# A gated scan followed by a mixture of experts: two norms on GpSimd, the first norm in one piece, and idle matrix time filled with unused products

## The chip, the cores and the metric

The kernel runs on one core of one Trainium2 chip. The metric is device time in microseconds (us), the median of several runs. Profiles are of one execution; TensorE is called PE, VectorE DVE, ScalarE ACT, GpSimd POOL and SyncE SP, as the profile calls them.

## The reference, cut to what matters

Input `x` has 4096 tokens of 128 channels, in 16 sequences of 256.

```python
# first half: a gated linear recurrence along each sequence
n  = layernorm(x)
it = sigmoid(n @ Wi.T + bi);  rt = sigmoid(n @ Wr.T + br)
at = exp(-8.0 * softplus(cap_lambda) * rt)
gx = sqrt(1.0 - at**2) * (it * n)
h[t] = at[t] * h[t-1] + gx[t]          # 256 steps, every channel by itself
x  = x + layernorm(h)
# second half: 32 experts, of which each token uses its 4 best
n  = layernorm(x)
scores = sigmoid(n @ gate_w.T)
ids    = top_k(scores + e_bias, 4);  w = scores[ids] / sum(scores[ids])
a[e]   = silu(n @ w1[e]) * (n @ w3[e]) * w[e]      # w1, w3: 128 x 96
x  = x + layernorm(sum over e of a[e] @ w2[e])     # w2: 96 x 128
```

## The kernel before

**Tiling.** The tokens are eight chunks (`CH`) of 512. For every chunk the piece `mix(c)` does the first half and the routing: normalise (`xn`), transpose (`xnT`), two gate products (`pr`, `pi`), the gates on ACT (`gr`, `gi`, `root`), the scan on DVE (`hs`), a transpose back (`back`), the norm `b`, the sum into `x_all`, the norm `c` (tile `hn`), a transpose (`hT`), the router product (`pl`), its scores and the choice of four experts.

**Two ways through the experts.** Six chunks, in the groups (0, 2, 3) and (4, 5, 6), go by tokens. `send` scatters the 512 x 4 rows of a chunk to the rows of their experts in DRAM with 16 indirect DMAs on POOL (`rows_in`, L507). When all 48 of a group are sent, `loads` brings blocks of 128 rows back on SP's queue (`xb`, L908), `experts` works on four blocks at a time (PE tiles `xT_ps`, `gu`, `aT_ps`, `y_ps`; ACT and DVE between them) and stores them (`rows_out`, L976). When all blocks of a group are stored, `fetch` gathers each token's four results with indirect DMAs on POOL (`yk`, L1044; 48 for a group), DVE weighs and adds them, and `combine` does the last norm and the store. Chunks 1 and 7 are dense: `dense(d, k)` runs all experts over a whole chunk in 24 blocks of 128 hidden units, products `dg`, `du`, `dw` (L1111) and `acc` (L1135), and `finish(d)` does the norm and the store (L1167). POOL's whole program is the setup at the start, the 96 scatters and the 96 gathers.

**The order.** Each piece is a Python generator that yields the engine and an assumed cost of its next step. `Order.run` takes, again and again, the step that can begin first on its own clock; among steps for one engine that begin within `SOON`, the one with the lowest due time goes first. This fixes the order of PE, DVE, ACT and SP; POOL's follows from it. Due times come from constants: chunk `c` is due at `LEAD + STEP * c`, experts from `full` on by `PACE`, dense blocks by `DUE` and `DDUE` (the last dense chunk by `DUE2`), always last on PE. `LND` and `CPD` are the assumed DVE costs where a step may go to ACT or DVE (`EITHER`); `STAY` puts off a step that makes ACT load another table. `AHEAD` goes into `in_pace`: a scatter or gather waits for the latest PE block product that the plan has at least `AHEAD` us earlier. `KEEP` is the number of blocks of the last dense chunk that may run before the last expert blocks have begun:

```python
        if d == len(DENSE) - 1 and k >= KEEP:
            yield UNTIL, lambda: 0.0 if began[-1] * QB >= NW[-1] else None
```

**The norms.** `rsqrt` is nine small DVE instructions (a shift-and-subtract guess and two Newton steps), each a step of its own, so others can be put between them. The first norm `a` has two pieces: `norm(range(1))` for chunk 0 and `norm(range(1, 8))` for the rest, and both are ready at once. For a name listed in `POWS`, `rsqrt` does an add and a power on POOL instead; the list is empty.

**Things in DRAM and weights.** SP's queue first loads `x_all`, clears the first group's rows, and then loads weights (`w`, `w_all`, `w_sb`) one piece after each of certain steps of `mix` (`some_later`).

Of the kernel before, what the change touches and what calls it, by code (L numbers as in the profile page):

```python
# [11 lines left out]
I32 = mybir.dt.int32  # L12
U32 = mybir.dt.uint32
AF = mybir.ActivationFunctionType
ALU = mybir.AluOpType
# [3 lines left out]
P = 128  # L19
EPS = 1e-5  # L20
K = 4
GROUPS = ((0, 2, 3), (4, 5, 6))
DENSE = (1, 7)
# [5 lines left out]
PE, DVE, ACT, POOL, SP, TIME = "pe", "dve", "act", "pool", "sp", "time"  # L29
# [7 lines left out]
class Order:  # L37
# [14 lines left out]
    def give(self, *names):  # L52
        for name in names:
            self.slots[name].append(self.now)
# [20 lines left out]
    def due(self, rank, step):  # L75
        due, n = rank
        if isinstance(due, dict):
            due = due.get(step[0], due[None])
        return due + STAY * self.switches(step), n

    def run(self, pieces):
# [8 lines left out]
        while live:  # L90
# [14 lines left out]
            if kind in (PE, DVE, ACT, POOL, SP):  # L105
                soon = [r for r in ready if r[3][0] == kind and r[0] <= begin + SOON]
                begin, _, p, step = min(soon, key=lambda r: self.due(r[1], r[3]))
# [19 lines left out]
                live.remove(p)  # L127


POWS = ()  # L130
POOLW = 0.9
RATE = 1.29
AHEAD = 3.0
READ = 0.0
LAST = 2
TINY = 0.07
SOON = 0.1
STAY = 6.0
LEAD, STEP, PACE = 38.0, 13.0, 0.6
DUE = 70.0  # L140
DDUE = 1.0
DUE2 = 200.0
LND, CPD = 1.7, 0.9
FLY2 = 3
KEEP = 6
MORE = 20
REGS = 3
SBANKS = 6
# [2 lines left out]
SLOT, UNTIL = "slot", "until"  # L151
# [3 lines left out]
def tile_gated_scan_then_moe(  # L155
# [30 lines left out]
    nc = tc.nc  # L186
# [3 lines left out]
    N = B * T  # L190
    TPC = 4
    CH = TPC * P
# [6 lines left out]
    NW = [min(n, t * K // P + MORE) for n, t in zip(NB, TG)]  # L199
    QB = 4  # L200
# [21 lines left out]
    def bank(name, dtype=F32):  # L222
        return psum.tile([P, CH], dtype, tag="bank", name=name)
# [128 lines left out]
    spread = const.tile([3 * E, UB * P], BF16, name="spread")  # L352
# [4 lines left out]
    for dst, src, rows in ((wiT, wi_in, P), (wrT, wr_in, P), (gwT, gw_in, E)):  # L357
# [5 lines left out]
    order = Order({  # L363
        "w": TILES - HELD, "ps": 8, "m": 3, "s": SBANKS, "d": 6, "acc": 2, "a": 4,
        "xb": 5, "regs": REGS, "blk": BLK, "yb": 4, "hn": HELD, "last": 3, "res": 1, "find": 2, "yk": 10,
    })
    give = order.give
# [11 lines left out]
    def rsqrt(rstd, var, pool, name):  # L379

        shape = [P, rstd.shape[1]]
        if name in POWS:
            v = pool.tile(shape, F32, tag="newt_v", name=f"nv_{name}")
            yield POOL, POOLW
            nc.gpsimd.tensor_scalar(v, var, EPS, None, ALU.add)
            nc.gpsimd.tensor_tensor(rstd, v, mhalf.to_broadcast(shape), ALU.pow)
            return  # L390
        v = pool.tile(shape, F32, tag="newt_v", name=f"nv_{name}")
        t = pool.tile(shape, F32, tag="newt_t", name=f"nt_{name}")
        yield DVE, TINY
        nc.vector.tensor_scalar(v, var, EPS, None, ALU.add)
        yield DVE, TINY
        nc.vector.tensor_scalar(
            t.bitcast(I32), v.bitcast(I32), 1, None, ALU.arith_shift_right
        )
        yield DVE, TINY
        nc.vector.tensor_scalar(  # L400
            rstd.bitcast(I32), t.bitcast(I32), -1.0, float(0x5F1FFFF9), ALU.mult, ALU.add
        )
        k = 0.703952253
        for square, plus in ((-1.0, 2.38924456), (-0.5 * k**3, 1.5 * k)):
            yield DVE, TINY
            nc.vector.scalar_tensor_tensor(t, rstd, square, rstd, ALU.mult, ALU.mult)
            yield DVE, TINY
            nc.vector.tensor_tensor(t, t, v, ALU.mult)
            yield DVE, TINY
            nc.vector.scalar_tensor_tensor(rstd, t, plus, rstd, ALU.add, ALU.mult)  # L410

    def moments(src, name, pool):

# [26 lines left out]
    times = {}  # L440
# [48 lines left out]
    def in_pace(ins):  # L489

        old = [b for at, b in beats if at <= order.now - AHEAD]
        if old:
# [6 lines left out]
    def send(g, cg):  # L499

        c = GROUPS[g][cg]
        yield UNTIL, lambda: times["rows", c][0] if ("rows", c) in times else None
        _, rows, hn = times["rows", c]
        for j in range(TPC):
            for k in range(K):
                yield POOL, RATE
                ins = nc.gpsimd.indirect_dma_start(  # L507
                    out=rows_in[g],
                    out_offset=bass.IndirectOffsetOnAxis(ap=rows[:, j, k : k + 1], axis=0),
                    in_=hn[:, j, :], in_offset=None,  # L510
                )
                apart(ins, f"in_{g}")
                in_pace(ins)
                sent[g].append(ins)
        times["sent", g] = order.now
        yield TIME, 2.5
        give("hn")
# [5 lines left out]

    def norm(chunks):

        for c in chunks:
            yield DVE, 1.1
            stats = small.tile([P, TPC, 6], F32, tag="stats_a", name=f"st_a{c}")
            for j in range(TPC):
                nc.vector.bn_stats(stats[:, j, :], x_all[:, c * TPC + j, :])  # L530
            for j in range(TPC):
                nc.vector.bn_aggr(mv_a[:, c * TPC + j, :], stats[:, j, :])
        span = slice(chunks[0] * TPC, (chunks[-1] + 1) * TPC)
        yield from rsqrt(rstd_a[:, span], mv_a[:, span, 1], const, f"a{chunks[0]}")
        yield DVE, TINY
        nc.vector.scalar_tensor_tensor(
            shift_a[:, span], mv_a[:, span, 0], -1.0, rstd_a[:, span], ALU.mult, ALU.mult
        )
        for c in chunks:
            times["normed", c] = order.now  # L540
# [8 lines left out]
    def decays():  # L549


        yield DVE, 0.4
        nc.vector.tensor_scalar(nabs, cap, -1.0, None, ALU.mult)
        nc.vector.tensor_tensor(nabs, nabs, cap, ALU.min)
        yield ACT, 0.2, "first exp"
        nc.scalar.activation(y, nabs, AF.Exp)
        yield DVE, 0.5
        nc.vector.tensor_scalar(u, y, 1.0, None, ALU.add)
        nc.vector.tensor_scalar(um1, u, 1.0, None, ALU.subtract)
        nc.vector.tensor_scalar(isz, um1, 0.0, None, ALU.is_equal)  # L560
        yield ACT, 0.2, "ln"
        nc.scalar.activation(lnu, u, AF.Ln)
        yield DVE, 1.2
        nc.vector.tensor_tensor(lnu, lnu, isz, ALU.add)
        nc.vector.tensor_tensor(um1, um1, isz, ALU.add)
        nc.vector.reciprocal(um1, um1)
        nc.vector.tensor_tensor(y, y, um1, ALU.mult)
        nc.vector.tensor_tensor(y, y, lnu, ALU.mult)
        nc.vector.tensor_scalar(decay, cap, 0.0, None, ALU.max)
        nc.vector.tensor_tensor(decay, decay, y, ALU.add)  # L570
        nc.vector.tensor_scalar(decay, decay, -4.0, None, ALU.mult)
        for b in (bi_sb, br_sb):
            nc.vector.tensor_scalar(b, b, 0.5, None, ALU.mult)
        times["decay"] = order.now
# [514 lines left out]
    def dense(d, k):  # L1089
# [3 lines left out]
        _, hT = times["hT", c]  # L1093
        if d == len(DENSE) - 1 and k >= KEEP:
            yield UNTIL, lambda: 0.0 if began[-1] * QB >= NW[-1] else None
# [75 lines left out]
    def spans(g, cg):  # L1171

        n = LAST if (g, cg) == (NG - 1, len(GROUPS[g]) - 1) else TPC
        return [(j, n) for j in range(0, TPC, n)]

    begun = set()
    w1_f, w3_f = (w13[:, i].rearrange("h e i -> h (e i)") for i in range(2))


    pieces = [(LEAD + STEP * c, mix(c)) for c in range(N // CH)]  # L1180
    pieces.append((0, norm(range(1))))
    pieces.append((-1, decays()))
    pieces.append((LEAD + STEP, norm(range(1, N // CH))))
    for g, chunks in enumerate(GROUPS):
        pieces += [(LEAD + STEP * c, send(g, cg)) for cg, c in enumerate(chunks)]
        full = LEAD + STEP * (chunks[-1] + 1)
        read = full + PACE * NW[g] + READ
        pieces.append((0, table(g)))
        pieces.append((0, loads(g, 0, NW[g])))
        pieces += [  # L1190
            (full + PACE * q, experts(g, q, NW[g])) for q in range(0, NW[g], QB)
        ]
        pieces += [
            (read + STEP * (cg + (j + n) / TPC), combine(g, cg, j, n))
            for cg in range(len(chunks)) for j, n in spans(g, cg)
        ]
        pieces += [(full + STEP * (cg + 1), find(g, cg)) for cg in range(len(chunks))]
        pieces += [
            (read + STEP * (cg + j / TPC), fetch(g, cg, j))
            for cg in range(len(chunks)) for j in range(TPC)  # L1200
        ]
    for d, c in enumerate(DENSE):
        pieces += [
            ({PE: 400 + d * UB + k, None: (DUE2 if d == len(DENSE) - 1 else DUE + DDUE * d * UB) + DDUE * k}, dense(d, k)) for k in range(UB)
        ]
# [13 lines left out]
    def step(piece, steps=None):  # L1219
# [14 lines left out]
    _, more_r = nc.values_load_multi_w_load_instructions(  # L1234
        more[0:1, 0:1], min_val=0, max_val=1,
        skip_runtime_bounds_check_because="0 or 1",
    )
# [42 lines left out]
```

## Time and profile before

| what | value |
|---|---|
| median of 3 runs | 376.28 us (375.01 to 378.33) |
| the profiled execution | 377.76 us, span 376.1 us |
| busy PE | 305.8 us (81%) |
| busy DVE | 290.7 us (77%) |
| busy ACT | 201.6 us (54%) |
| busy POOL | 195.4 us (52%) |
| mean granted PE clock | 0.927 |
| scatters on POOL, 96 | 66.3 to 213.5 us |
| gathers on POOL, 96 | 229.8 to 364.0 us |
| block loads on SP, 136 | 136.0 to 277.7 us |
| last store begins | 371.5 us |

A row of the timeline has the start and the length in us, the engine (with a q for its queue), the line of the kernel, the operation, output and inputs, the shapes, how many instructions are merged, and in brackets how long the engine was idle before and what ended that. A row of the stages has the stretch, its length, each engine's busy time and number of instructions, the granted PE clock (1 is full), and the DMA share and rate. PE ends are modelled.

### The profile page before, as it was taken

How to read it: one execution, taken by the hardware profiler on the slowest of the kernel's cores; microseconds unless marked ns; L12 is line 12 of the kernel's file. 1: busy time of each engine (PE TensorE's matmuls, PEld its weight loads, DVE VectorE, ACT ScalarE, POOL GpSimd, SP SyncE). 2: the span in 40 equal slices, each digit the busy share in tenths (PEclk: the TensorE clock that was granted, in tenths of full speed). 3: DMA queues.
4: the chain of work that ended last, by engine and by line, in shares of the span. 5: the costliest groups of instructions: out<-in, count | busy, mean ns of one | idle time of the engine just before them, and what ended most of it. 6: DMA issues, size and time to landing. Idle time of an engine off the chain costs nothing.

```text
span 376.1 us, 6098 instructions
## 1 busy us (share of the span) xinstructions
PE 305.8 (81%) x1423; PEld 199.2 (53%) x1423; DVE 290.7 (77%) x1252; ACT 201.6 (54%) x376; POOL 195.4 (52%) x220
## 2 busy tenths in 40 slices
PE   1095479799999998888889989877999999999900
PEld 0051254354543446777889956766999644444300
DVE  6955996989899998877874799637367488796993
ACT  2289897688677415457565546545466523141210
POOL 5000000772777727656737504776377767777750
PEclk9998657699999999899999999999699999999975
DMA  6906678362111124455545255667374522122231
GB/s 150 315 0 183 195 207 200 99 195 84 45 56 49 56 72 141 140 161 173 160 133 155 75 166 158 181 182 196 89 200 121 161 69 78 52 56 77 56 101 31
DMA packets 78856, 47.16 MB, mean 125 GB/s; under 512 B 15296, under 2 KB 75744, under 8 KB 78816
## 3 DMA queue, kind: packets, MB, share of 16 engines
q1 hardware_dynamic: 53808, 25.05, 24.3%
q0 software_dynamic: 6144, 12.60, 11.8%
q10 hardware_dynamic: 18864, 9.08, 8.2%
q8 instruction: 13, 0.21, 0.2%
q14 instruction: 27, 0.22, 0.2%
HBM read 23.76 MB, written 22.94 MB: 124 GB/s over the span
## 4 chain that ended last, share of the span: by engine, by line
PE 62%; DVE 12%; issue 5%; ACT 3%; POOL 2%; DMA 1%; DVEq 0%; POOLq 0%
PE gu L938 12%; PE acc L1135 10%; PE dg L1111 8%; PE y_ps L964 8%; PE du L1111 8%; PE aT_ps L954 4%; PE xT_ps L924 4%; PE dw L1111 2%; PE pl L675 2%; POOL yk L1044 2%; DMA yk<-rows_out,slots 1%; DVE a L1131 1%; DVE a L1123 1%; PE pr L600 1%; PE sw_c L448 1%
## 5 line engine op out<-in xcount | busy, mean ns | idle before, releaser
L507 POOL DMA_INDIRECT rows_in<-hn,rows x96 | 94.9, 988 | 113.2 <-DVE tot L481 60.8
L1044 POOL DMA_INDIRECT yk<-rows_out,slots x96 | 95.7, 996 | 54.8 <-issue 17.4
L938 PE MATMUL gu<-w,xT 128*128 x272 | 53.8, 336 | 7.9 <-issue 6.4
L1120 ACT ACTIVATE a<-dg 128x512 f32<-128x512 f32 x48 | 28.4, 596 | 49.7 <-PE dg L1111 49.2
L1135 PE MATMUL acc<-a,w_all 128*128 128x512 f32 x96 | 50.5, 617 | 3.3 <-DVE a L1131 1.4
L938 PEld LDWEIGHTS gu<-w,xT 128*128 128x128 f32 x272 | 44.6, 194 | 12.4 <-issue 7.7
L1111 PE MATMUL dg<-hT,w 128*128 128x512 f32 x96 | 50.7, 614 | 0.0
L1111 PE MATMUL du<-hT,w 128*128 128x512 f32 x96 | 50.0, 606 | 0.0
L946 DVE TENSOR_TENSOR act<-act,gu 128x192 f32<-128x192 f32 x68 | 23.0, 349 | 23.0 <-ACT act L944 22.5
L964 PE MATMUL y_ps<-w_sb,aT 96*128 x272 | 36.2, 280 | 5.3 <-issue 3.2
L1131 DVE TENSOR_TENSOR a<-a,dw 128x512 f32<-128x512 f32 x48 | 32.5, 681 | 9.1 <-PE dw L1111 8.6
L964 PEld LDWEIGHTS y_ps<-w_sb,aT 96*128 96x128 f32 x272 | 34.5, 196 | 8.5 <-issue 7.5
L1123 DVE TENSOR_TENSOR a<-a,du 128x512 f32<-128x512 f32 x48 | 32.4, 678 | 4.9 <-ACT a L1120 3.3
L944 ACT ACTIVATE act<-gu 128x192 f32<-128x192 f32 x68 | 22.0, 330 | 25.8 <-PE gu L938 21.6
L973 ACT COPY yb<-y_ps 128x512 f32<-128x512 f32 x34 | 19.9, 586 | 23.3 <-PE y_ps L964 22.3
L1135 PEld LDWEIGHTS acc<-a,w_all 128*128 128x128 f32 x96 | 17.1, 195 | 23.9 <-DVE a L1131 9.2
L1111 PEld LDWEIGHTS dg<-hT,w 128*128 128x128 f32 x96 | 18.3, 196 | 19.0 <-issue 17.3
L1111 PEld LDWEIGHTS du<-hT,w 128*128 128x128 f32 x96 | 17.7, 195 | 15.5 <-issue 14.0
L954 PE MATMUL aT_ps<-ident,act 128*96 128x128 f32 x136 | 20.4, 279 | 2.3 <-issue 1.6
L370 ACT COPY aT<-aT_ps 96x512 f32<-96x512 f32 x29 | 16.6, 583 | 9.4 <-PE aT_ps L954 8.1
L1054 DVE TENSOR_TENSOR yk<-yk,wk 128x512 f32<-128x512 f32 x24 | 16.5, 688 | 6.2 <-DMA yk<-rows_out,slots 6.0
L370 ACT COPY xT<-xT_ps 128x512 f32<-128x512 f32 x29 | 16.7, 588 | 7.0 <-PE xT_ps L924 6.1
(215 smaller groups left out, 520.9 us busy)
## 6 DMA issues: line engine op xcount, KB each, us to landing
xb<-rows_in SPq DMA_DIRECT2D x136, 64.0 KB
rows_out<-yb ACTq DMA_DIRECT2D x34, 256.0 KB
rows_in<-zeros SPq DMA_DIRECT2D x8, 512.0 KB
w<-in_L_ffn_w_dram SPq DMA_DIRECT2D x8, 384.0 KB
x_all<-in_L_attn_x_dram SPq DMA_DIRECT2D x8, 256.0 KB
w_all<-in_L_ffn_w_dram SPq DMA_DIRECT2D x4, 384.0 KB
w_sb<-in_L_ffn_w_dram SPq DMA_DIRECT2D x4, 384.0 KB
rows_in<-hn,rows POOLq DMA_INDIRECT x96
```

The lines of the kernel that those rows point to most:

```text
L370: (nc.vector.tensor_copy if kind == DVE else nc.scalar.copy)(dst, src)
L507: ins = nc.gpsimd.indirect_dma_start(out=rows_in[g], out_offset=bass.IndirectOffsetOnAxis(ap=rows[:, j, k : k + 1], axis=0), in_=hn[:, j, ...
L938: nc.tensor.matmul(pg[:, b, :], lhsT=xT[:, (h + b) * P : (h + b + 1) * P], rhs=w13[:, :, bass.ds(e, 1), :].rearrange("h s o i -> h s (o i) ...
L946: nc.vector.tensor_tensor(act[:, h : h + m, :], act[:, h : h + m, :], pg[:, :m, I : 2 * I], ALU.mult)
L954: nc.tensor.transpose(pa[:I, b * P : (b + 1) * P], act[:, b, :], ident)
L964: ins = nc.tensor.matmul(py[:, b, :], lhsT=aT[:, b * P : (b + 1) * P], rhs=w2_sb[:, bass.ds(e, 1), :].rearrange("i o h -> i (o h)"), start ...
L1044: ins = nc.gpsimd.indirect_dma_start(out=yk[:, k, :], out_offset=None, in_=rows_out[g], in_offset=bass.IndirectOffsetOnAxis(ap=rows[:, j, ...
L1111: ins = nc.tensor.matmul(ps, lhsT=lhsT, rhs=rhs, start=True, stop=True)
L1120: nc.scalar.activation(a, pg, AF.Silu)
L1123: nc.vector.tensor_tensor(a, a, pu, ALU.mult)
L1131: nc.vector.tensor_tensor(a, a, pw, ALU.mult)
L1135: nc.tensor.matmul(accs[d], lhsT=w2_all[:, k, :], rhs=a, start=(k == 0), stop=(k == UB - 1))
```

## The change

Two norms of the dense chunk 1 (`b1`, `c1`) go to POOL as powers. For chunk 0's norm `a` the nine instructions are one step, and the norm of the other chunks begins only after it. A new piece `warm` issues matrix products (96 x 128 by 96 x 512 in bf16) into one PSUM bank, which nothing reads, wherever the plan has PE idle, until the plan's clock is at 45. The last dense chunk's `mix` is due at 200 instead of 129, none of its blocks may go ahead of the last expert blocks, and several constants of the order differ. `LATER` is zero and changes nothing.

```diff
-POWS = ()
-POOLW = 0.9
+POWS = ("b1","c1")
+ATONCE = ("a0",)
+POOLW = 1.4
-AHEAD = 3.0
+AHEAD = 5.0
+WARM = 45.0
+MIXD = 200.0
+LATER = 0.0
-SOON = 0.1
-STAY = 6.0
-LEAD, STEP, PACE = 38.0, 13.0, 0.6
-DUE = 70.0
-DDUE = 1.0
+SOON = 0.12
+STAY = 8.0
+LEAD, STEP, PACE = 38.0, 11.0, 0.6
+DUE = 62.0
+DDUE = 2.0
-LND, CPD = 1.7, 0.9
+LND, CPD = 1.1, 0.7
-KEEP = 6
+KEEP = 0
...
+        def steps():
+            nc.vector.tensor_scalar(v, var, EPS, None, ALU.add)
+            yield
...                          # the same nine instructions as before
+        if name in ATONCE:
+            yield DVE, 1.7
+            for _ in steps():
+                pass
+            return
         yield DVE, TINY
+        for _ in steps():
             yield DVE, TINY
...
     def norm(chunks):
+        if chunks[0]:
+            yield UNTIL, lambda: times.get(("normed", 0))
...
+    def warm():
+        yield SLOT, "ps"
+        ps = bank("warm")
+        while order.now < WARM:
+            yield PE, 0.22
+            nc.tensor.matmul(
+                ps, lhsT=spread[:, :P], rhs=spread[:, :CH], start=True, stop=True
+            )
+        give("ps")
...
-    pieces = [(LEAD + STEP * c, mix(c)) for c in range(N // CH)]
+    pieces = [
+        (MIXD if c == DENSE[-1] else LEAD + STEP * c, mix(c)) for c in range(N // CH)
+    ]
+    pieces.append((1e6, warm()))
...
-            (full + PACE * q, experts(g, q, NW[g])) for q in range(0, NW[g], QB)
+            (full + PACE * q + LATER * g, experts(g, q, NW[g])) for q in range(0, NW[g], QB)
```

More of the change, by code (lines that the diff above doesn't have):

```diff
@@ L392, in rsqrt @@
         t = pool.tile(shape, F32, tag="newt_t", name=f"nt_{name}")
-        yield DVE, TINY
[L394 to L404, printed above, removed]
-            yield DVE, TINY
[L406 to L410, printed above, removed]
+        def steps():
+            nc.vector.tensor_scalar(v, var, EPS, None, ALU.add)
+            yield
+            nc.vector.tensor_scalar(
+                t.bitcast(I32), v.bitcast(I32), 1, None, ALU.arith_shift_right
+            )
+            yield
+            nc.vector.tensor_scalar(
+                rstd.bitcast(I32), t.bitcast(I32), -1.0, float(0x5F1FFFF9), ALU.mult, ALU.add
+            )
+            k = 0.703952253
+            for square, plus in ((-1.0, 2.38924456), (-0.5 * k**3, 1.5 * k)):
+                yield
+                nc.vector.scalar_tensor_tensor(t, rstd, square, rstd, ALU.mult, ALU.mult)
+                yield
+                nc.vector.tensor_tensor(t, t, v, ALU.mult)
+                yield
+                nc.vector.scalar_tensor_tensor(rstd, t, plus, rstd, ALU.add, ALU.mult)
+        if name in ATONCE:
[3 more added lines that the diff above has]
+            return
+        yield DVE, TINY
+        for _ in steps():
+            yield DVE, TINY
     def moments(src, name, pool):
@@ L1174, in spans @@
         return [(j, n) for j in range(0, TPC, n)]
+    def warm():
[5 more added lines that the diff above has]
+                ps, lhsT=spread[:, :P], rhs=spread[:, :CH], start=True, stop=True
+            )
+        give("ps")
     begun = set()
     w1_f, w3_f = (w13[:, i].rearrange("h e i -> h (e i)") for i in range(2))
-    pieces = [(LEAD + STEP * c, mix(c)) for c in range(N // CH)]
+    pieces = [
+        (MIXD if c == DENSE[-1] else LEAD + STEP * c, mix(c)) for c in range(N // CH)
+    ]
     pieces.append((0, norm(range(1))))
     pieces.append((-1, decays()))
+    pieces.append((1e6, warm()))
     pieces.append((LEAD + STEP, norm(range(1, N // CH))))
```

## The prediction

> **What bounds the kernel now.** I read the page's slices first, then the timeline of the start and of the end, then tables by stage.
>
> ```profile
> PE   1095479799999998888889989877999999999900
> DVE  6955996989899998877874799637367488796993
> ACT  2289897688677415457565546545466523141210
> POOL 5000000772777727656737504776377767777750
> ```
>
> A slice is 9.4 us. PE is nearly full from about 70 us to 358; the chain of waits gives PE 62% of the span. Before 70 us PE is not the bound: ACT is, from 20 to 60 us (37.6 us busy of 40 by stages). POOL is idle until its first scatter at 66.3. So what the start loses, the full PE stretch begins later by.
>
> ```profile
> 9.70 0.16 DVE L394 TENSOR_SCALAR nv_a<-mv_a 128x4 f32<-128x4 f32 x1
> 9.77 0.87 DVE L530 BATCH_NORM_STATS2 st_a<-x_all 128x6 f32<-128x128 f32 x4
> ...
> 17.31 0.16 DVE L536 SCALAR_TENSOR_TENSOR shift_a<-mv_a,rstd_a 128x4 f32<-128x4 f32 x1
> 17.51 1.65 ACT L377 ACTIVATE xn<-x_all,shift_a,rstd_a 128x128 f32<-128x128 f32 x4 [6.77 <-DVE shift_a L536]
> ...
> 25.26 0.69 ACT L607 ACTIVATE gr<-pr,br_sb 128x512 f32<-128x512 f32 x1
> ```
>
> Chunk 0's nine small instructions are strung out from 9.70 to 17.3 because the statistics of the other chunks (0.87 + 0.37 us each) stand between them; ACT waits 6.77 us for the end of it, and the first gate comes at 25.26.
>
> ```profile
> 34.30:44.50 10.20, 5.59 (x11) 2.27 (x10) 8.95 (x48) 9.93 (x14) 0.00 (x0) 0.50 0.73 203
> 44.50:47.90 3.40, 2.14 (x6) 0.57 (x5) 3.40 (x22) 1.97 (x5) 0.00 (x0) 1.00 0.68 196
> 47.90:61.60 13.70, 11.10 (x31) 6.99 (x31) 11.41 (x59) 13.53 (x19) 0.00 (x0) 0.50 0.94 239
> 61.60:68.40 6.80, 4.78 (x23) 2.14 (x21) 5.39 (x39) 2.71 (x6) 1.79 (x2) 1.00 0.31 90
> 68.40:75.20 6.80, 6.06 (x12) 2.70 (x13) 6.48 (x32) 4.80 (x8) 5.11 (x6) 0.50 0.42 127
> ```
>
> The stages show a PE at half clock in three stretches, the second being where the dense blocks begin.
>
> ```profile
> 56.34 3.76 PE L1111 MATMUL dg<-hT,w 128*128 128x512 f32 x4
> 59.89 2.73 PE L1111 MATMUL du<-hT,w 128*128 128x512 f32 x4
> 62.97 0.29 DVE L761 TENSOR_TENSOR places<-rank,filled 128x128 f32<-128x128 f32 x1 [3.15 <-PE rank L757]
> ```
>
> Chunk 0's ranking, which its first scatter needs, stood behind eight dense products that took 6.1 us instead of 3.4 (a pair at full clock is 0.86 in the chain).
>
> ```profile
> 303.16 0.94 POOL L1044 DMA_INDIRECT yk<-rows_out,slots  x1 [2.06 <-PE dw L1111]
> 363.09 0.95 POOL L1044 DMA_INDIRECT yk<-rows_out,slots  x1 [0.30 <-issue]
> 365.24 0.37 SPq L1167 DMA_DIRECT2D out_dram<-res  x1
> 371.48 0.37 SPq L1082 DMA_DIRECT2D out_dram<-ff  x1
> ```
>
> The end: the last group's blocks are stored at about 300, then 48 gathers at 1.25 to 1.27 us fill POOL to 364, and 12 us of weighing, norm and store follow. The last dense chunk's store begins 6.24 us ahead of the last one: that is its slack.
>
> **The change part by part.** Minus is earlier.
>
> *First norm.* Statistics of chunk 0 end at 6.75. The same nine instructions in a row take 1.75 us for norm b (36.67 to 38.42), so 8.5; three steps for the decay wait for ACT until 9.26 and end at 9.8; the shift ends at 10.0. With the lower assumed cost the scaling goes to DVE: eight took 2.14, so four 1.07, to 11.1. Transposes trail by 0.5, the copy is 0.6, the gate product at half clock 2.1: first gate at about 14.5, so -10.8 for chunk 0. The other chunks' statistics start later for it. DVE's work to the end of that norm is the same, less some 0.7 idle, plus the scaling 1.07 and chunk 0's early steps 2.6, so it ends near 23.5 instead of 20.7; with 3.5 us for scaling, transpose, copy and product, the next gate comes near 27 instead of 32.7. ACT has chunk 0's 6.8 us (0.69 + 0.82 + 0.71 + 0.64 + 0.72 + 0.63 and two table loads of 1.28) behind it by then. Bounds for the start of the dense blocks: 0, if ACT catches nothing up, to -10.8; I take -6, nearest to the second chunk's 5.7.
>
> *Powers.* Each takes nine DVE instructions (1.75) away and puts two on POOL, which is idle there. No power is in the trace. POOL's smallest rows are a memset of 0.10, the nearest of more work the two copies of 128x32 in 1.80: a norm costs 0.2 to 1.8, the two gain 3.1 to lose 0.1. I take 0.9 each, so 1.7 on chunk 1's chain, and count -1, as ACT is the bound there. If POOL were no longer idle, they would stand behind scatters of 1.26 us.
>
> *Unused products.* A pair of the like (`dw`) is 0.60, so one more costs 0.22, or 0.43 at half clock. The plan lays one per 0.47 us where PE has no other work; they delay a real product by 0.43 at most each, in a stretch that ACT bounds: cost 0, up to +1 if a bunch stands before a late transpose. They take one of eight banks until the dense blocks. Gain: 3.0 us at 56 to 62 if the clock is then full (eight products, 6.1 against 3.4, and the rank behind them), and as much as 2.7 more at 68 to 75, which they don't reach directly. Bounds -5.7 to +1; I take -3.
>
> The stages show what PE's clock needs: 81% busy from 47.9 to 61.6, much of it transposes and narrow products, and still half. [...]
>
> *KEEP and MIXD.* By tile, three blocks' `dg` and `du` and one `acc` of the last dense chunk ran from 213.5 to 291:
>
> ```profile
> 213.50:291.00 77.50, 2.96 (x6) 1.06 (x6) 1.70 (x3) 0.96 0.58 158
> 291.00:360.00 69.00, 21.45 (x42) 7.97 (x42) 12.50 (x21) 1.00 0.29 79
> ```
>
> (`dg`; 48 more instructions before.) That is 3 x 1.72 + 0.86 and some `dw`, 6.5 us of PE, moved behind the last group's blocks. Ahead of them it is worth -6.5 at most and nothing where it filled a wait; PE was 92% busy from 213.5 to 228, so I take -3. At the end it costs +6.5 against 6.24 of slack, so +0.3; up to +6.5 if DVE, 83% busy there (48.28 of 58.2), stretches it. Chunk 7's mixing, done at 226 until now, may slide; DVE has 28 us idle from 228 to 300, so I cost it at nothing.
>
> *AHEAD and the due times.* Scatters and gathers wait 8.3 and 14.7 us for PE products; 2 us of slack each can take away some of it. But the first group's gathers start when its blocks are stored, and the second's likewise, so 0, bounds -4 to +4 together with the changed dues, whose order no row shows.
>
> **Sum.** -6 - 1 - 3 - 3 = -13 for PE's full stretch. Not all reaches the end: PE carries 62% of the chain; the rest are other engines' steps and waits, the gathers at their own pace among them, that I leave as long as they are. So -13 x 0.62 = -8.1, +0.3, or -7.8: span 368.3, the profiled execution 370.0. That execution was 1.48 above the median, so the median becomes 368.5; I say 368.
>
> **The rivals.**
>
> *All of it arrives.* PE full from 60 on, looser pacing: -13 and -4, 359 to 363. For it: PE 93% busy from 70 to 213.5 (133.68 of 143.5). Against: gathers of the first group, 229.8 to 301, are the floor of the second's start; 48 at 1.25 leave only 11 us there.
>
> *The gain is given back.* Earlier scatters only wait longer for the next chunk's rows (POOL already waits 6.6 us at 94 and 6.2 at 140), as DVE (68.77 of 75.1 us busy from 75 to 150) sets chunks 2 to 6: 374 to 378. For it: DVE work falls by 3.5 us only.
>
> *The dense end decides, slower.* All 24 blocks of the last chunk need its `hT` and routing, and its `mix` now yields to everything until 200. A block is 0.86 x 3 + 0.22 = 2.8 us, 24 of them 67, the norm and store 7.3 + 4.6. If chunk 7 is ready later than the last expert blocks begin (about 291), each us goes to the end: 10 us late is 376.1 + 10 + 0.3, or 386. It decides from 4 us late on. Against: it would have to slide 65 us from 226.
>
> *Powers behind scatters.* If chunk 1's second norm comes after chunk 0's scatters are queued, it waits up to 16 x 1.26 = 20 us and the dense blocks start 13 later than now: 385. Now 15 us lie between (51 and 66.3); chunk 0 gains some 5 on chunk 1, so 10 remain. [...]
>
> **How the numbers follow.** Forecast 0.49 (its own range 362 to 374), all of it 0.18, given back 0.18, dense end 0.11, powers 0.04. A change under 1% (3.8 us) can't be told from none. Faster by over 1%, below 372.5: 0.67, all of the second and the forecast's. Within 1%: 0.18. Slower: 0.15, the last two. The range reaches from 358, past the largest gain, to 381, where the dense end is some 5 us late.
>
> **What would show it.** The first gate at 14 to 16; no half clock from 48 to 62; first dense product near 48; first scatter below 58; last scatter near 204, last gather near 355. Wrong if the first scatter moves by 8 or more and the last one stays at 213, or if `res` is the last store.

## The result, and the profile after

The changed kernel takes 379.58 us (median of four runs, 378.89 to 383.44), the one before beside it 376.73. The ratio is 1.011, with a 95% interval of 1.0065 to 1.0156: slower by 1.1%, where the prediction had it 2.1% faster. The profiled execution took 378.89 us with a span of 376.9.

Some executions are slower than the rest at a lower granted clock (of a_high, one took 382.82 us at 0.915 and one 374.23 at 0.945); a median here takes in all executions of a kernel and a ratio leaves those out, so that one median divided by another need not give the ratio.

The slices of the page of after:

```profile
PE   1998678999999688959799869777989999999940
DVE  7998899899889998947488986556858787888993
ACT  2599975876941124527355335434666332112110
POOL 5000187337557775174377037745666477777700
```

POOL starts its scatters two slices earlier than before. DVE is fuller at both ends (303.5 us busy against 290.7), ACT emptier (180.2 against 201.6). PE has more dips between 50 and 300 us.

The start, in the timeline of after (start, length, engine, line, operation):

```profile
8.88 5.30 PE L1198 MATMUL warm<-spread 96*128 96x512 bf16 x12
9.76 0.15 DVE L552 SCALAR_TENSOR_TENSOR shift_a<-mv_a,rstd_a 128x4 f32<-128x4 f32 x1
9.94 1.12 DVE L379 TENSOR_SCALAR xn<-x_all,rstd_a,shift_a 128x128 f32<-128x128 f32 x4
...
13.97 1.06 PE L462 MATMUL sw_a<-ident,xn 128*128 128x128 f32 x4
...
16.97 0.69 ACT L623 ACTIVATE gr<-pr,br_sb 128x512 f32<-128x512 f32 x1
```

The shift comes at 9.76 (17.31 before), the scaling lies on DVE, and the first gate comes at 16.97 instead of 25.26. Between the end of the scaling (11.06) and the transposes (13.97) lie 2.9 us; twelve unused products occupy PE from 8.88 to 14.18.

POOL, and the two DVE rows that compute where the next chunk's rows go, in the timeline of after:

```profile
42.83 1.05 POOL L393 TENSOR_TENSOR rs_b<-nv_b,mhalf 128x4 f32<-128x4 f32 x1
...
47.21 1.47 POOL L393 TENSOR_TENSOR rs_c<-nv_c,mhalf 128x4 f32<-128x4 f32 x1
48.88 1.25 POOL L521 DMA_INDIRECT rows_in<-hn,rows  x1 [0.21 <-issue]
...
79.63 0.17 DVE L490 TENSOR_SCALAR rows<-most 128x16 int32<-128x16 f32 x1
80.57 0.96 POOL L521 DMA_INDIRECT rows_in<-hn,rows  x1 [10.75 <-PE dg L1127]
...
157.38 0.17 DVE L490 TENSOR_SCALAR rows<-most 128x16 int32<-128x16 f32 x1
158.31 0.95 POOL L521 DMA_INDIRECT rows_in<-hn,rows  x1 [10.84 <-PE xT_ps L940]
```

The two powers are done before the first scatter, which starts at 48.88, 17.4 us earlier than before. Then POOL waits 10.8 us, twice. Nearly all of it is for the next chunk's row numbers (`rows`, ready at 79.8 and 157.6); the last 0.8 us are for the PE product that the written order has ahead of the scatter. The last scatter of the second group ends at 207.8, only 5.7 us earlier.

Two tables by stage of after (stretch, length, busy time and instructions of PE, weight load, DVE, ACT and POOL, clock, DMA share, GB/s):

```profile
47.90:59.77 11.87, 10.38 (x27) 6.10 (x28) 11.54 (x63) 8.44 (x13) 9.28 (x9) 0.57 0.84 215
...
210.00:240.00 30.00, 22.64 (x128) 17.86 (x127) 22.88 (x82) 11.74 (x24) 13.83 (x14) 0.94 0.51 137
240.00:295.00 55.00, 49.33 (x353) 46.07 (x352) 36.54 (x136) 29.78 (x65) 32.59 (x35) 0.97 0.62 169
```

Where the dense blocks begin the clock is again near half (0.57). Their first product stands at 53.87, against 56.34. From 210 to 295 PE is idle for (30 - 22.64) + (55 - 49.33) = 13.0 us; before it was 8.7 in the same stretches.

The end, in the timeline of after:

```profile
357.88 1.04 POOL L1060 DMA_INDIRECT yk<-rows_out,slots  x1 [0.31 <-issue]
...
362.49 1.12 PE L1151 MATMUL acc<-a,w_all 128*128 128x512 f32 x2 [1.19 <-DVE a L1147]
...
368.17 0.37 SPq L1098 DMA_DIRECT2D out_dram<-ff  x1
...
369.04 1.37 DVE L379 TENSOR_SCALAR res<-ff,rs_d,sh_d 128x128 f32<-128x128 f32 x4
372.77 0.69 DVE L1181 TENSOR_TENSOR res<-res,x_all 128x512 f32<-128x512 f32 x1 [2.37 <-DVEq L1268]
373.49 0.37 SPq L1183 DMA_DIRECT2D out_dram<-res  x1
```

This is the main reading. The kernel has two ends: the tokens' (last gather, then an `ff` store) and the dense one (last `acc`, then the `res` store of chunk 7). Before, the tokens' end was last: gathers to 364.0, `ff` at 371.5, `res` at 365.2. After, gathers end at 358.9 and `ff` is stored at 368.2, earlier by 5.1 and 3.3 us; but the last `acc` ends at 363.6 instead of 357.1, and `res` is stored at 373.5, later by 8.3. **The gain reached the tokens' end, and the dense end took its place.**

### The profile page after: what moved, and what is told of

The parts are those of the page before. It is cut to its first block, busy times and chain, and to the rows that moved or that the text cites. A ratio compares the mean times of both kernels' runs of the same rounds, so it can differ in the third digit from the quotient of the medians.

```text
span 376.9 us, 6241 instructions
## 1 busy us (share of the span) xinstructions
PE 317.0 (84%) x1488; PEld 205.9 (55%) x1488; DVE 303.5 (81%) x1278; ACT 180.2 (48%) x329; POOL 195.7 (52%) x224
## 5 line engine op out<-in xcount | busy, mean ns | idle before, releaser
L1060 POOL DMA_INDIRECT yk<-rows_out,slots x96 | 93.0, 969 | 58.1 <-issue 16.8
L954 PE MATMUL gu<-w,xT 128*128 x272 | 56.0, 347 | 11.6 <-issue 11.4
L954 PEld LDWEIGHTS gu<-w,xT 128*128 128x128 f32 x272 | 47.0, 203 | 14.3 <-issue 13.2
L1151 PEld LDWEIGHTS acc<-a,w_all 128*128 128x128 f32 x96 | 16.2, 189 | 29.1 <-DVE a L1147 20.4
L940 PE MATMUL xT_ps<-ident,xb 128*128 128x128 f32 x136 | 20.6, 281 | 1.3 <-issue 1.3
L970 PEld LDWEIGHTS aT_ps<-ident,act 128*96 128x96 f32 x136 | 16.0, 133 | 8.7 <-issue 5.6
L374 ACT COPY aT<-aT_ps 96x512 f32<-96x512 f32 x24 | 13.6, 584 | 14.4 <-PE aT_ps L970 14.1
```

The costliest lines, as they stand in the source:

```text
L954: nc.tensor.matmul(pg[:, b, :], lhsT=xT[:, (h + b) * P : (h + b + 1) * P], rhs=w13[:, :, bass.ds(e, 1), :].rearrange("h s o i -> h s (o i) ...
L970: nc.tensor.transpose(pa[:I, b * P : (b + 1) * P], act[:, b, :], ident)
L1060: ins = nc.gpsimd.indirect_dma_start(out=yk[:, k, :], out_offset=None, in_=rows_out[g], in_offset=bass.IndirectOffsetOnAxis(ap=rows[:, j, ...
L1151: nc.tensor.matmul(accs[d], lhsT=w2_all[:, k, :], rhs=a, start=(k == 0), stop=(k == UB - 1))
```

## The experiments

For each run: the ratio of its time to that of the kernel before, run beside it on the same chip, and times of its profiled execution, in us. A 95% interval is the range in which the ratio lies by the scatter of the executions. The profiled executions of a_oldlnd_keep6, b_newlnd and a_high were some 2.5 us above their medians, those of a_near1 and a_near2 2.3 and 3.2 us below, so their ends are late or early by some of that.

| kernel | ratio (95%) | first `dg` | last gather ends | last `acc` ends | `ff` store | `res` store | busy DVE / ACT |
|---|---|---|---|---|---|---|---|
| before | 1 | 56.3 | 364.0 | 357.1 | 371.5 | 365.2 | 291 / 202 |
| after | 1.011 (1.0065 to 1.0156) | 53.9 | 358.9 | 363.6 | 368.2 | 373.5 | 304 / 180 |
| a_keep6 | 1.0113 (1.007 to 1.0156) | 53.9 | 361.3 | 357.2 | 370.9 | 365.6 | 305 / 181 |
| a_oldlnd | 0.9887 (0.9853 to 0.992) | 52.5 | 353.4 | 356.3 | 362.8 | 363.4 | 292 / 195 |
| a_oldlnd_keep6 | 0.9824 (0.9773 to 0.9875) | 52.5 | 358.5 | 355.5 | 367.2 | 363.1 | 292 / 197 |
| a_lnd_only | 1.0006 (0.997 to 1.0042) | 52.9 | 358.1 | 361.5 | 368.0 | 368.6 | 299 / 190 |
| b_newlnd | 1.0253 (1.0202 to 1.0305) | 56.0 | 373.8 | 372.2 | 384.6 | 381.4 | 306 / 185 |
| a_frozen | 1.0221 (1.0176 to 1.0266) | 55.5 | 363.6 | 369.0 | 373.5 | 378.7 | 292 / 190 |
| o_frozen | 0.9879 (0.9821 to 0.9938) | 52.5 | 355.4 | 358.3 | 364.8 | 365.4 | 302 / 185 |
| a_near1 | 1.0197 (1.0146 to 1.0249) | 73.4 | 348.5 | 367.1 | 359.8 | 376.2 | 300 / 182 |
| a_near2 | 0.9923 (0.9887 to 0.9958) | 57.7 | 352.0 | 357.3 | 362.1 | 364.6 | 286 / 199 |
| a_high | 1.004 (1.0004 to 1.0076) | 57.9 | 364.1 | 364.2 | 373.7 | 373.0 | 284 / 208 |

**Parts undone or done alone.** The first theory was that `KEEP = 0` had made the dense end last, and that this was the loss.

```diff
 a_keep6, from after
-KEEP = 0
+KEEP = 6
```

> The changed kernel with KEEP back at 6 and nothing else undone. Theory 1 (the dense chunk's end decides: its 24 blocks stand behind the last expert blocks, and its last add behind the branch): three or more of its blocks go ahead again, its last store comes 6 us or more earlier, a store of ff is the last one, and the median is 374 to 376, 4 to 6 below the changed kernel's 379.6. Theory 2 (the gain of the start is given back before the end, between scatters and gathers): within 1.5 us of 379.6.

The time stayed: 378.97 us, 1.0113. Its end in the timeline:

```profile
360.34 0.94 POOL L1060 DMA_INDIRECT yk<-rows_out,slots  x1 [0.30 <-DMA yk<-rows_out,slots]
...
365.61 0.37 SPq L1183 DMA_DIRECT2D out_dram<-res  x1
370.88 0.37 SPq L1098 DMA_DIRECT2D out_dram<-ff  x1
```

The dense end did come back, its last `acc` by 6.4 us, but the last gather went 2.4 later and `ff` 2.7. What `KEEP` gives one end it takes in part from the other. Alone it decides nothing, and without it all the rest of the change moves the last store only from 371.5 to 370.9. So more than the dense end was wrong.

```diff
 a_silent, from after: the products are in the plan, and not issued
-            nc.tensor.matmul(
-                ps, lhsT=spread[:, :P], rhs=spread[:, :CH], start=True, stop=True
-            )
+            if order.now < 0.0:
+                nc.tensor.matmul(
+                    ps, lhsT=spread[:, :P], rhs=spread[:, :CH], start=True, stop=True
+                )
```

> The changed kernel with the same written order, in which the 65 unused products are planned but not issued; all real instructions keep their places. If the products earn their place by the clock: half clock again from about 30 to 48, first scatter 1 to 4 us later than 48.9, median 380 to 383. If they only stand in the way of real products: first scatter earlier by 1 or more, median 377 to 379. If PE does not bound the start: within 1 us of 379.6, first scatter within 1 us.

380.33 us, 1.0125 (1.0081 to 1.0169): not to be told from after. The first gate came earlier without the products (14.9, against 17.0), the first scatter later (50.6, against 48.9). From 34 to 50 us the mean clock was 0.67 without them and 0.98 with them; from 50 to 62, where the dense blocks begin, 0.59 and 0.60. They buy a full clock where they run and none behind it.

```diff
 a_nobranch, from after
-    with tc.If(more_r[0] > 0):
...                               # the fallback code at the end is left out
```

> The changed kernel without the branch at the end (the code for blocks beyond the planned number, which these inputs don't need, is left out). Theory 1: the last add of the dense chunk follows its scaling directly instead of 2.4 us later, and the median is 376 to 377.5, 2 to 3.5 below 379.6; gathers and everything before 360 unchanged. If the end of the program costs as much without the branch: within 1 us of 379.6.

378.74 us, 1.0117 (1.0062 to 1.0172). The gap of 2.4 us in front of the last addition (`DVEq L1268`) belongs to this code: without it `res` is stored 7.5 us behind the last `acc`, against 9.9. But taking it away gained nothing that can be told: the last `acc` came 2.0 us later in this run, and `res` was stored at 373.1 instead of 373.5.

```diff
 b_norm, from before: only the first norm in one step, and the order of the two pieces
+ATONCE = ("a0",)
...
+        if chunks[0]:
+            yield UNTIL, lambda: times.get(("normed", 0))
```

> The kernel before with only the first norm's change (nine instructions in one step, the other chunks' norm after it); all constants as before. If the early start carries through by itself: first gate at 16 to 19 instead of 25.3, first scatter 5 to 10 us earlier than 66.3, median 370 to 374. If it is given back at the later waits: first gate early all the same, first gathers of the second group within 2 us of 303, median 375.5 to 378.

379.86 us, 1.0122 (1.0077 to 1.0166). The first gate was at 14.4 and the first scatter at 48.1, but the first dense product at 64.6, 8.3 later than before: chunk 0's further steps now come ahead of chunk 1's, whose `hT` moved from 54.0 to 62.3 as chunk 0's moved from 48.7 to 37.4. The last gather ended at 364.7, no earlier than before. The largest term of the prediction, taken alone, is a loss.

```diff
 a_keep24_mixd, from after
-MIXD = 200.0
+MIXD = 115.0
-KEEP = 0
+KEEP = 24
```

> The changed kernel with KEEP at 24 (no block of the last dense chunk is held back) and chunk 7's mixing due at 115, as its number would give, instead of 200. Theory A (PE's work bounds the stretch up to the last expert blocks, and what is held back lengthens the end): the blocks fill PE where it idled in the changed kernel (25 us from 120 to 300), 5 or more of them leave the end, the last accumulation comes 10 us or more before the last gather, and the median is 372 to 376. Theory B (the end is set by the gathers and DVE, whatever PE does): blocks move, but the median stays within 1.5 of 379.6.

386.32 us, 1.017 (1.0114 to 1.0227). Three of chunk 7's blocks had their `dg` and `du` from 223.3 to 234.4, where after has none before 285.4. They filled little idle time: from 50 to 295 us PE is idle for 28.2 us, against 29.2 in after. The last scatter came 5.0 us later (212.8), the last gather 11.1 (370.0). The 5.0 are not the blocks' doing, as the scatters end before the first of them; chunk 6's `hn` already came 5.0 later (162.0, against 157.0). Two constants change here at once, so how much each costs is not told apart.

```diff
 a_dense_first, from after: chunk 1 due one us before chunk 0
-        (MIXD if c == DENSE[-1] else LEAD + STEP * c, mix(c)) for c in range(N // CH)
+        (MIXD if c == DENSE[-1] else LEAD - 1 if c == DENSE[0] else LEAD + STEP * c, mix(c)) for c in range(N // CH)
```

> The changed kernel with the dense chunk 1 due before chunk 0 (37 instead of 49). Theory A (PE-bound from the first dense product on, so that the dense chunk's start counts and chunk 0's scatters don't): first dense product 4 to 8 us earlier than 53.9, first scatter 4 to 10 us later than 48.9, and still the last expert store 2 to 5 us earlier than 294.8 and the median 375 to 377.5. If the scatters are the path: last expert store and median later by 3 or more, 382.5 and up.

380.05 us, 1.0104 (1.0064 to 1.0144), and the first dense product at 54.8, later by 0.9: the due time does not bring chunk 1 forward.

**The two assumed costs.** Of the constants, `LND` and `CPD` are what decides whether a scaling or a copy goes to ACT or DVE. A first run changed `LND` alone, and only for the last norms:

```diff
 a_dact, from after
-        kind = yield EITHER, 0.4 * n, LND * n / TPC
+        kind = yield EITHER, 0.4 * n, (1.7 if kind == "d" else LND) * n / TPC
```

> The changed kernel in which only the last norms' scaling is planned with the old DVE cost, so that it goes to ACT in the last 130 us. Theory C (DVE, 85% busy in the end, stretches both the dense chain and the last gathers' norms): 1.1 us less DVE work per chunk, the last store 2 to 4 us earlier, median 375.5 to 377.5; scatters and everything before 240 within 0.5 us. If DVE has room there: within 1 of 379.6.

377.44 us, 1.0055 (1.0024 to 1.0086): by the ratios about 2 us better than after, though the two intervals overlap. Then both costs, everywhere:

```diff
 a_oldlnd, from after
-LND, CPD = 1.1, 0.7
+LND, CPD = 1.7, 0.9
```

> The changed kernel with the assumed DVE costs as before (LND 1.7, CPD 0.9). Theory C (13 us of copies and scalings went from ACT to DVE, and DVE is a second bound): DVE busy falls from 303 to about 292, ACT rises to 195, the median is 374 to 377. If only PE and the gathers bound: DVE falls all the same and the median stays within 1.5 of 379.6.

371.01 us, 0.9887 (0.9853 to 0.992). This one line turns the change from 1.1% slower to 1.1% faster. Both ends come early (`ff` 362.8, `res` 363.4), and the copies go back to ACT (194.5 us busy, DVE 291.6). From the other side, in the kernel before:

```diff
 b_newlnd, from before
-LND, CPD = 1.7, 0.9
+LND, CPD = 1.1, 0.7
```

> The kernel before with one line changed, the assumed DVE costs 1.1 and 0.7 in place of 1.7 and 0.9. Theory (these two numbers load DVE, which is the second bound, and that is what turned the gain of the other parts into a loss): DVE busy goes from 291 to 300 or more, ACT from 202 to under 190, and the time is 381 to 386, 1.5 to 3% slower. Rival (they do harm only together with the earlier start and the later chunk 7, as part of one order that happened to be bad): within 1% of before, 373 to 379.

388.32 us, 1.0253 (1.0202 to 1.0305): the two numbers alone cost the old kernel more than the whole change did. And half of it:

```diff
 a_lnd_only, from after
-LND, CPD = 1.1, 0.7
+LND, CPD = 1.7, 0.7
```

> The kernel after with the assumed cost of four scalings back at 1.7 and that of a copy left at 0.7. If the scalings (four 128x128 pieces on DVE, 1.1 to 1.4 us) are what loads DVE, nearly all of the 8.6 us comes back: 371 to 373. If it is the copies (0.69 each), under a third: 376 to 379. Between: both share.

375.46 us, 1.0006 (0.997 to 1.0042): a little under half of the way, so by these two runs both numbers share. (How far one order can stand for a pair of costs comes below.)

**Load or order.** That the two numbers do it is shown; the reason that I gave, that they load DVE, is another matter. Two kernels move copies from one engine to the other at the moment of writing, and leave the written order as it is.

```diff
 a_frozen, from after (22 copies that the plan has on DVE; so too for aT)
-        copy(kind, xT[:, : nb * P], pt[:, : nb * P])
+        copy(ACT, xT[:, : nb * P], pt[:, : nb * P])
```

> The kernel after with its written order untouched; only the engine of the 22 copies xT and aT in the token blocks that the plan had laid on DVE is changed to ACT at the moment of writing, so DVE has 22 x 0.69 = 15 us less and ACT 22 x 0.59 = 13 us more. Theory of load: busy DVE about 288, ACT about 193, as with the old assumed costs, and the time comes most of the way, 371 to 375. Rival (it is the order that the plan writes with the old costs, not the load): no gain, 378 to 382, as the copies only come later behind ACT's own list.

```diff
 o_frozen, from a_oldlnd (19 copies that the plan has on ACT; for aT with == 1)
-        copy(kind, xT[:, : nb * P], pt[:, : nb * P])
+        copy(DVE if q // QB % 3 == 0 else kind, xT[:, : nb * P], pt[:, : nb * P])
```

> The kernel after with the old assumed costs (371.0 us), its written order untouched on PE, POOL and SP; 19 of the 58 copies xT and aT of the token blocks that ACT has are written to DVE instead, so DVE busy rises from 291.6 to about 304, that of after. Theory of load: the time goes to 378 to 382, that of after. Theory of order: it stays within 370 to 374, or moves by the 1 to 2 us that copies out of their planned place cost.

The pages' busy times, first of a_oldlnd, then of o_frozen:

```profile
PE 314.6 (85%) x1486; PEld 202.6 (55%) x1486; DVE 291.6 (79%) x1245; ACT 194.5 (53%) x363; POOL 196.8 (53%) x224
```

```profile
PE 318.8 (86%) x1486; PEld 206.1 (56%) x1486; DVE 301.6 (81%) x1264; ACT 184.6 (50%) x344; POOL 197.2 (53%) x224
```

With 10 us more on DVE and 10 less on ACT, o_frozen has nearly after's load and still a_oldlnd's time: 0.9879 against 0.9887. And a_frozen, with the load of a_oldlnd in after's order (DVE 291.7, ACT 190.3), is slower than after: 384.52 us, 1.0221. **For the copies the load theory falls: what remains is the order that the plan writes with these costs.** Copies moved against a written order gained nothing in either run.

One load is left out of this test. In after 18 of the 24 pieces of the tokens' last norms (`ff`) and all eight of the dense ones (`res`) are scaled on DVE, 7.7 us; in a_oldlnd and o_frozen alike it is 4 and 4, 2.5 us. No run moves these scalings in a fixed order, so whether their 5 us at the two ends count as load is **not settled**; a_dact, which puts most of them back on ACT, also writes a new order.

**How much an order varies.** Three more pairs of costs, in after:

```diff
-LND, CPD = 1.1, 0.7
+LND, CPD = 1.15, 0.72     # a_near1
+LND, CPD = 1.8, 0.95      # a_near2
+LND, CPD = 2.3, 1.1       # a_high
```

> The kernel after with assumed costs of 1.15 and 0.72 in place of 1.1 and 0.7. If the size of the two numbers decides, it is as after, 378 to 381. If each order is good or bad by chance, it can lie anywhere from 370 to 384, and a step of over 3 us away from after's 379.6 shows that.

> The kernel after with assumed costs of 1.8 and 0.95 in place of the old 1.7 and 0.9. If their size decides, as with the old ones, 369 to 373. If by chance, anywhere from 368 to 384, and over 3 us from 371 shows it.

> The kernel after with assumed costs of 2.3 and 1.1. The trend so far is 379.6 at 1.1 and 0.7, 375.5 at 1.7 and 0.7, 371.0 at 1.7 and 0.9. If higher assumed costs of DVE go on to help: 366 to 371, with DVE busy below 290. If 1.7 and 0.9 is near the best because ACT then waits: 371 to 376.

383.53 us (1.0197), 373.49 (0.9923) and 377.63 (1.004). A step of 3 to 6% in the two numbers made the time longer both times, by 0.9% (a_near1 against after) and by 0.4% (a_near2 against a_oldlnd, where the intervals overlap), and no trend goes on at the upper end. So one order is worth some tenths of a per cent by itself, up to about 1%. Yet the groups stay apart: in the changed kernel 1.1/0.7 and its neighbour give 1.011 and 1.0197, 1.7/0.9 and its neighbour 0.9887 and 0.9923. The end of a_near1 is the clearest picture of the two ends:

```profile
347.57 0.94 POOL L1060 DMA_INDIRECT yk<-rows_out,slots  x1 [0.30 <-DMA yk<-rows_out,slots]
...
365.96 1.13 PE L1151 MATMUL acc<-a,w_all 128*128 128x512 f32 x2 [0.78 <-DVE a L1147]
...
376.20 0.37 SPq L1183 DMA_DIRECT2D out_dram<-res  x1
```

Its gathers end at 348.5, 10.4 us earlier than in after and 15.5 earlier than before, and it is slower than both: its first dense product comes only at 73.4, the dense end at 367.1, and `res` is the last store, 16.4 us behind the last `ff`. That the late start made the late end is likely, and no run shows it.

```diff
 a_oldlnd_keep6, from after
-LND, CPD = 1.1, 0.7
+LND, CPD = 1.7, 0.9
-KEEP = 0
+KEEP = 6
```

> The kernel after with the old assumed costs 1.7 and 0.9 and with six blocks of the last dense chunk allowed ahead of the last expert blocks. If the dense end decides now that DVE is relieved (the res store began last, 363.4 against 362.8): 367 to 370. If KEEP's price is nothing, as it was alone: 370 to 373. If the blocks delay the last expert blocks, whose stores release the gathers: 374 or more.

371.12 us, 0.9824 (0.9773 to 0.9875): the interval overlaps that of a_oldlnd, so `KEEP`'s price is nothing that can be told, as it was alone. Its profiled execution has the last `ff` later (367.2, against 362.8) and `res` where it was (363.1), but as it was 2.4 us above the median, that `KEEP` moves the tokens' end here too is not shown.

**Three dense blocks fewer.** The last pair asked which end sets the time, without another order.

```diff
 a_less, b_less: three blocks of chunk 7 are planned, and not issued
+        left = d == 1 and 18 <= k <= 20
...
-        nc.scalar.activation(a, pg, AF.Silu)
+        if not left:
+            nc.scalar.activation(a, pg, AF.Silu)
...                     # so too for the products and the two DVE steps
```

> The kernel after without blocks 18 to 20 of the last dense chunk (their five products and three DVE and ACT instructions each are left out, so the result of that chunk lacks them); everything else in its written order. Three blocks are 3 x 2.8 = 8.4 us of PE in the last 70 us. Theory: the dense end sets the time of after (res is the last store, 373.5, against 368.2 for the tokens), so the last acc product comes about 8 us earlier and the time falls by the 5.3 us between the two stores: 373 to 375. Rival (DVE, which both ends share, or the gathers set it): the tokens' store stays last or near it, and the time falls by less than 2 us: 378 or more.

> The kernel before without the same three blocks of the last dense chunk. Theory: the tokens' end sets the time there (ff store 371.5, res 365.2), so 8.4 us of PE less give at most the 1 to 2 us by which DVE is freed for the weighing: 374 to 376. Rival (PE sets the time in both): 368 to 371.

These two ran on a chip on which the kernel before itself took 433.94 us, so they are read only against that. b_less took 435.21 us, 1.0053 (0.9993 to 1.0113). Three blocks less gave the old kernel nothing; its last store was still `ff` (429.8, `res` 423.8). That agrees with the tokens' end as the old kernel's bound. a_less took 451.56 us, 1.0489 (1.0407 to 1.0571), its last store still `res` (459.2, `ff` 453.9, in a profiled execution 12.7 us above the median). No run of after stands beside it there, so what the blocks cost after is **not settled** by it; that the dense end is after's last rests on the order of the stores alone.

## Why the prediction was wrong, point by point

**The step that failed** is the price of the changed order: "so 0, bounds -4 to +4 together with the changed dues, whose order no row shows". The two assumed costs, which write that order too, got no term at all; I used them only for one scaling ("With the lower assumed cost the scaling goes to DVE"). They measured 2.2% of the time, or 8.4 us (1.011 against 0.9887), twice the bound. With them put back, the rest of the change gains 1.1%, 4.2 us, where the sum said 7.8: the sign was right for the rest, and the size a little over half. As neighbouring orders differ by up to 0.9%, some of either number is the luck of the one order that was written.

**KEEP and MIXD.** Both halves were priced well: -3 ahead measured -2.4 at the last gather, and +6.5 at the end measured +6.4 at the last `acc` (after against a_keep6). What failed is "so +0.3", from 6.24 us of slack. It took for granted that whatever came early would bring both ends forward alike. The rest of the change brought the tokens' stores 0.6 us forward (a_keep6 `ff` 370.9 against 371.5) and the dense end not at all (last `acc` 357.2 against 357.1), so the 6.4 us fell on an end with no gain, and another 1.7 came between `acc` and the store (9.9 us, against 8.1).

**First norm.** The first gate was to come at 14.5 and came at 17.0; without the unused products it is 14.9. "-10.8 for chunk 0" holds to within 2.5, and the first scatter, 17.4 us earlier, beat the forecast. The term in the sum was -6 at the start of the dense blocks; with the powers and the unused products it was to be -10, and all of the change together brought -2.5. The step "ACT has chunk 0's 6.8 us ... behind it by then" overlooked that chunk 0's own later steps move forward too and stand in front of chunk 1's: b_norm shows +8.3 for the norm by itself.

**Powers.** 0.9 us a norm was taken from bounds of 0.2 to 1.8; add and power take 1.28 for b and 1.71 for c. They stood behind no scatter. No run has the powers alone, so their -1 is not measured. From the end of the statistics (42.42) to the end of the first power (43.88) it is 1.5 us.

**Unused products.** -3 was mis-sized: 0.15% between after and a_silent, 0.6 us, within the noise. Its condition, a full clock at 56 to 62, was shown by no row of before, and the products did not bring it about: from 50 to 62 the clock was 0.60 with them and 0.59 without. "They delay a real product by 0.43 at most each" missed that the plan lays many in a row: the first transposes stood behind twelve. And the clock where the dense blocks begin is half as before, 0.57 from 47.90 to 59.77. By single microseconds it is full to 49, half from 50 to 59 and full from 60 on. In front of the fall PE had 2.7 us without a product (45.96 to 48.62); the last unused products stand at 41.05. The full clock came back about 5.7 us after the first dense product (`dg`, 53.87); in before it took about 5.2 us (from 56.34), in a_silent about 4.4 (from 55.5, by the mean of 0.59 from 50 to 62). This PE was 87% busy from 47.90 to 59.77 (10.38 of 11.87 us), and counted from 50.3, where transposes and narrow products begin to fill it without a gap, the full clock took 9.3 us to come back. What sets the fall and the return is not shown.

**"So -13 x 0.62"** scaled the gain of the start by PE's share of the chain. The profile has no such proportion. POOL's scatters gained 17.4 us at the first and 5.7 at the last, as they waited 10.8 us twice, nearly all of it for rows: my rival "the gain is given back" described that way rightly. The rival "the dense end decides" named the right end and the wrong cause: chunk 7's `hT` was ready at 235.4, 50 us before the first product that reads it (285.4), and its routing (`combT`) at 282.0, 12.9 us before its first (294.9). Its "from 4 us late on" also disagrees with the sum, where +0.3 makes the dense end the last one with no lateness at all.

**The marks.** First scatter below 58: yes. First gate at 14 to 16, no half clock from 48 to 62, first dense product near 48, last scatter near 204, last gather near 355: no (17.0, half, 53.9, 207.8, 358.9). "Wrong if `res` is the last store": it is.

**What stays open** is which steps of the order make PE wait. In the list of PE's own waits from 50 to 364 us the sums grew most for two:

```profile
PE gu L954 <- issue: 11.4, 4, 4.3
PE acc L1151 <- DVE a L1147: 8.7, 10, 3.2
```

These are after's; before, they were 6.4 and 1.4 us, and in a_oldlnd 7.3 and 5.1. From 50 to 295 us PE is idle for 22.6 us before, 29.2 after and 25.4 in a_oldlnd, by the tables of stages. That the two costs are the cause was shown from both sides, and that the copies' load is not; that these two waits are how the order acts was only read off the lists. Open too are the last norms' scalings, and `AHEAD`, `SOON`, `STAY`, `STEP`, `DUE` and `DDUE`, none of which was tried alone.

## What to carry to other kernels

In a kernel whose order is written by a planner, a constant of the planner is an edit of every instruction behind it: give it a term of its own with a bound of some per cent, and try each constant alone before a change of mechanism is judged by it. Where two chains end near each other, follow a gain to each of the two ends; slack between them holds only if both are moved alike. An assumed cost near the measured time (a DVE copy takes 0.69 us, and 0.7 was assumed) is not for that reason the better one: 0.9 wrote the faster order.

## What the runs showed of the hardware that was not expected

The two powers of a 128x4 tile on GpSimd took 1.05 and 1.47 us, and the adds of one immediate on the same tiles 0.23 and 0.24. With products of no use in it PE had nearly the full clock from 34 to 50 us (0.98, against 0.67 without them), and in the 12 us behind them 0.60, though by the profile it was busy for 11.68 of those 12. Last, one chip ran the unchanged kernel in 434 us instead of 376. In b_less's timeline there, PE stopped in the midst of full stretches, for 3.21 us before 118.37 and for 2.92 before 140.59; the first:

```profile
118.37 1.10 PE L1115 MATMUL dg<-hT,w 128*128 128x512 f32 x2 [3.21 <-remote]
```

What held it up is not shown.
